# Two attention blocks: layer 1's value product by halves twice, and the late differences of the exponentials moved

## The chip, the cores and the metric

The kernel runs on one core of one Trainium2 chip. The metric is the device time of one execution in microseconds (us); a kernel is given by the median of its runs. A core has five engines that run side by side and wait for each other through semaphores: TensorE (PE, matmuls, into the accumulator memory PSUM), VectorE (DVE), ScalarE (ACT), GpSimd (POOL[...]) and SyncE (SP, which here issues the DMAs).

## What is computed

Eight images of 512 channels and 32 x 32 = 1024 positions ("tokens") go through two attention blocks one after the other. The reference, cut to what matters:

```python
# layer 0: 8 heads of 64 channels, group norm over 32 groups
h = group_norm(x, gn_weight, gn_bias)
q, k, v = split(einsum('oc,bct->bot', w_qkv, h) + b_qkv)      # by head
weight = softmax(einsum('bct,bcs->bts', q * scale, k * scale))
x = x + einsum('oc,bct->bot', w_proj, einsum('bts,bcs->bct', weight, v)) + b_proj
# layer 1: one head of 512 channels, group norm over 8 groups
xn = group_norm(x, gamma, beta)
q, k, v = (conv1x1(xn, w, bias) for w, bias in ((q_w, q_b), (k_w, k_b), (v_w, v_b)))
attn = softmax(einsum('bqc,bck->bqk', q^T, k) * c ** -0.5)
x = x + conv1x1(einsum('bqk,bkc->bqc', attn, v^T)^T, p_w, p_b)
```

All is float32.

## The kernel before

**Products by halves.** Most large products use a Winograd form of Strassen's scheme: both factors are cut into 2 x 2 blocks, seven products of sums of blocks take the place of eight, and the results are added up on the way out of PSUM. `left_sums` (L151) and `right_sums` (L165) make the sums of a left and a right factor. `wino` (L227) runs one such level: steps 1, then 6, 2, 5, 7, then 4 and 3. Steps 4 and 3 are put into the list `tail` and run by `finish` (L223) after step 1 of the next product, so that results are not waited for. `conv2` (L503) divides in halves twice: seven outer products, each of seven inner ones, 49 instead of 64. It takes the outer products in four pairs, (1, 5), (2, 6), (7,), (3, 4), and `inner_steps` (L434) runs the inner steps 1, 6, 2, 5, 7 of a pair, and 3 and 4 as its tail after the next pair's step 1. In the later pairs the results of earlier ones are added in (`x`), and in the third pair POOL adds blocks of the output to each other (`more`, L534).

**PSUM.** Three tags, a, b and c, have two buffers each. In `inner_steps` steps 1 and 2 of a pair share one buffer of a, steps 6, 7 and 4 one of b, steps 5 and 3 one of c. Step 6 adds onto a copy of step 1's result; DVE or ACT must have read b after step 6 before step 7 adds to it.

**Layer 1.** The query and key weights are multiplied into one matrix m, the value and projection weights into one matrix z, in the prologue. For each image `layer1_scores` (L997) forms g = m x image by `conv2`. `layer1_rest` (L1007) then does three stages:

1. `scores1` (L666): the scores by halves twice. DVE evicts, ACT takes the exponential in place (`exps`, L695), POOL adds up the exponentials (`add_up`, L699; the result is `total`). Eight difference operations on whole tiles of exponentials (`steps` of `right_sums`; in the profile `t<-e,e`, `t<-e,t` and `e<-e,e` on L742) make the right factor of the values. The first four run on DVE, the last four on POOL.
2. z: `by_token` (L361), one level of halves, tokens on the partitions. A step has eight matmuls with 256 moving columns. Its weight sums are one tile `w_z`. Hooks after its steps hold the next group norm's mean (`gmean`, `d`, `dv`) and its scale (`gvar`, `ve`), and `sums`, which multiplies `total` with ones, inverts it (`rc`) and sends it round by DMA as rows `r`.
3. `values1` (L746): exponentials times z, one level of halves, with 512 moving columns. It ends with the residual and the store. During this stage the next image's factors `inner_h` are made on POOL and `t_h` on DVE.

**What sets the order.** TensorE's instructions stay in the program's order. Small operations wait in a list `background`; `run_background` takes one per inner step, or a few per step of `wino`. The eight difference operations are put on that list by the last product of the scores, whose tail runs behind z's step 1. Operations that are not pinned may be moved within their engine by the scheduler[...].

**Layer 0's v** is made by the same `conv2` with `by_tokens=True` from the second image on.

**Weights.** The sums of one level are kept in DRAM by `keep` (one DMA), those of two levels by `keep2`, which first makes four more sums (on POOL, `prepare_...` 128x896) and then stores seven parts. `load_weight` loads the next weight tile of a fixed list `uses`; three tiles fit. p and z are prepared during the first image's attention of layer 0.

The lines that matter most:

```python
            def step(j):
                ...
                elif j == 6:
                    mm(ps["b"], 6, False)
                    put([keep_tmp("u2", "u")], "b", (0, 1))
                ...
                elif j == 7:
                    mm(ps["b"], 7, False)
```

Of the kernel before, what the change touches and what calls it, by code (L numbers as in the profile page):

```python
# [9 lines left out]
F32 = mybir.dt.float32  # L10
# [5 lines left out]
P = 128  # L16
EPS = 1e-5
ORDER = (1, 5, 2, 6, 7, 3, 4)
NBIG = 32

# [7 lines left out]
def two_attention_blocks_kernel(  # L30
# [8 lines left out]
    nc = tc.nc  # L39
    B, C, T = x.shape  # L40
    KC = C // P
    HT = T // 2
# [41 lines left out]
    dram = ctx.enter_context(tc.tile_pool(name="dram", bufs=1, space=bass.MemoryType.DRAM))  # L84
# [91 lines left out]
    def main_path(ctx):  # L176
# [8 lines left out]
        def big_tile(name, shape=(P, T)):  # L185
            return big.tile(list(shape), F32, tag="big", name=name)

        def pair_tile(name):
            return big_tile(name, (P, 2, HT))
# [23 lines left out]
        background = []  # L213
# [76 lines left out]
        def keep(n, t):  # L290
            nc.sync.dma_start(wdram[n], t)


        wdram2 = {n: dram.tile([P, 7, 7, P], F32, name=f"sums2_{n}") for n in "qkmv"}

        def keep2(n, t, engine=nc.gpsimd):

# [16 lines left out]
        twice = {n: [(n, 0), (n, 1)] for n in wdram2}  # L314
        layer0 = [*twice["v"], *twice["k"], *twice["q"]]
        uses = ["p", *layer0] if B > 1 else ["p"]
        for b in range(1, B):
            uses += ["p", *twice["m"], "z"] + (layer0 if b + 1 < B else [])
        uses += [*twice["m"], "z"]
        loaded = []  # L320

        def load_weight():
# [18 lines left out]
        def weight(n):  # L341
            return weight_factors(weight_part(n))
# [323 lines left out]
        def scores1(f, gf, gsteps, first, uid, stats):  # L666

            scale = C**-0.5
            e = {(c, cc, r): pair_tile(f"e_{uid}_{c}{cc}{r}") for r in range(2) for c in range(2) for cc in range(2)}
            total = pair_tile(f"sum_{uid}")
            parts = [pair_tile(f"sum{r}_{uid}") for r in range(2)]
            g2 = {1: first}

            def factors(p):
                g2[p] = query_factors(gf[p], f"{p}_{uid}")

            def blocks(at, r, cc):
                return [e[at[1], cc, at[0]][:, :, ts(r, 2 * P)]]

            def add(dst, ps, x):
                nc.vector.tensor_add(dst[0], ps, x[0])  # L685

            def more(dst, x, y, r, cc):

                tc.keep_in_program_order(
                    nc.gpsimd.tensor_tensor(blocks(dst, r, cc)[0], blocks(x, r, cc)[0], blocks(y, r, cc)[0], ALU.add)  # L690
                )

            def exps(r, c):
                for cc in (1, 0):
                    nc.scalar.activation(e[c, cc, r], e[c, cc, r], AF.Exp, scale=scale)  # L695

            def add_up(r, c):

                on = lambda dst, x, y: lambda: tc.keep_in_program_order(nc.gpsimd.tensor_tensor(dst, x, y, ALU.add))  # L699
                if r == c:  # L700
                    return [on(parts[r], e[c, 0, r], e[c, 1, r])]
                return [
                    *(on(parts[r], parts[r], e[c, cc, r]) for cc in range(2)),
                    on(total[:, r, :], parts[r][:, 0, :], parts[r][:, 1, :]),
                ]

            def product(s, p, y, x, before, small, after7=(), final=()):
                def mm(ps, j, start):
                    for i in range(2):
                        matmul(  # L710
                            ps[:, i, :], f[p][j][:, ts(i, P)], g2[p][j], start=start and i == 0, stop=True, skip_group_check=True
                        )

                def extra(r, cc, read, written):

                    if p == 6 and written:
                        more((0, 1), (1, 0), (1, 1), r, cc)
                    if p == 7 and written:
                        more((1, 1), (1, 0), (1, 1), r, cc)

                inner_steps(
                    f"{uid}_{s}", s % 2, 2, mm, add, lambda *at: blocks(y, *at), x and (lambda *at: blocks(x, *at)),
                    extra, after7, final, [lambda: background.extend(small), *(lambda q=q: factors(q) for q in before)],
                )

            product(0, 1, (1, 0), None, [2], stats[:3] + gsteps[:2])
            product(1, 2, (0, 0), (1, 0), [5], gsteps[2:4], (), [lambda: exps(0, 0)])
            product(2, 5, (1, 1), None, [6, 4], gsteps[4:] + stats[3:5])
            product(3, 6, (1, 0), (1, 0), [7, 3], [])
            product(4, 7, (1, 0), (1, 0), [], stats[5:7])  # L730
            product(5, 3, (0, 1), (0, 1), [], stats[7:10] + add_up(0, 0), [lambda: exps(1, 1)], [lambda: exps(0, 1)])
            product(
                6, 4, (1, 0), (1, 0), [], stats[10:] + add_up(1, 1) + add_up(0, 1), (),
                [lambda: exps(1, 0), lambda: background.extend(add_up(1, 0) + steps)],
            )

            t = [[pair_tile(f"t{n}_{uid}_{cc}") for cc in range(2)] for n in (1, 2, 4)]
            engines = [nc.vector] * 4 + [nc.gpsimd] * 4
            fs, steps = right_sums(
                [(e[0, cc, 0], e[0, cc, 1]) for cc in range(2)], [(e[1, cc, 0], e[1, cc, 1]) for cc in range(2)],  # L740
                [lambda cc, n=n: t[n][cc] for n in range(3)],
                lambda *a: engines.pop(0).tensor_tensor(*a, ALU.subtract),  # L742
            )
            return total, {p: [x[:, i, :] for x in fs[p] for i in range(2)] for p in fs}

        def values1(b, zf, ef, r, xt, uid, hooks):  # L746
            def mm(p, i, ps, start):
                for k in range(4):
                    matmul(
                        ps, zf[p][k // 2][:, k % 2, ts(i, P)], ef[p][k], start=start and k == 0, stop=k == 3, skip_group_check=True  # L750
                    )

            def done(i, row, c, ps, u):
                oc = 2 * row + i
                o = upool.tile([P, HT], F32, tag="o", bufs=2, name=f"o_{uid}_{oc}_{c}")
                if u is None:
                    nc.vector.tensor_mul(o, ps, r[:, c, :])
                else:
                    nc.vector.tensor_add(o, ps, u)  # L759
                    nc.vector.tensor_mul(o, o, r[:, c, :])  # L760
                xh = xt[oc][:, ts(c, HT)]
                nc.vector.scalar_tensor_tensor(xh, o, obias[1][:, oc : oc + 1], xh, ALU.add, ALU.add)
                nc.sync.dma_start(out[b, oc * P : (oc + 1) * P, ts(c, HT)], xh)

            wino(f"av_{uid}", mm, done, middle=(2, 5, 6, 7), hooks=hooks, back=4)
# [60 lines left out]
        def prologue():  # L826
# [3 lines left out]
            first = {n: prepare(n) for n in "vqk"}  # L830
# [40 lines left out]
            norm1.affine(acc_tile("gvar_0_1")[:, :KC])  # L871
            bias = bias_products([(wk, "bq1"), (raw_p, "bv1"), (raw_p0, "bv0")])
            later = []
            for n in "pz":
                t, steps = prepare(n)
                later.append(steps)
                later.append([lambda n=n, t=t: keep(n, t), load_weight])
            later.append([
                lambda: tc.keep_in_program_order(nc.vector.tensor_copy(ubias, bias[0])),
                lambda: tc.keep_in_program_order(nc.vector.tensor_add(obias[1], bias[1], pcols("bp1"))),  # L880
# [125 lines left out]

        def layer1_rest(b, inner, gf, gsteps, stats, hooks, ahead):  # L1007
            first = query_factors(gf[1], f"1_1_{b}")
            total, ef = scores1(inner, gf, gsteps, first, f"1_{b}", stats)
            state = {}  # L1010

            def sums():
                state["r"] = reciprocals(total, f"1_{b}", True)

            z = by_token(
                weight("z"), hf, f"z1_{b}", hooks=[*hooks, [sums]], back=3,
                after=[load_weight, lambda: background.extend(zsteps)],
            )
            all_background()
            xt = [load_again(b, c, "x") for c in range(KC)]  # L1020
            stiles = [big_tile(f"sz{i}_{b}", (P, 2, 2, C // 2)) for i in (1, 2, 4)]
            halves = lambda t: (t[:, :, : C // 2], t[:, :, C // 2 :])
            zf, zsteps = left_sums(
                [halves(t) for t in z[:2]], [halves(t) for t in z[2:]],
                [lambda j, t=t: t[:, j, :, :] for t in stiles], nc.vector.tensor_add, nc.vector.tensor_sub,
            )
            values1(b, zf, ef, state["r"], xt, f"1_{b}", ahead)

        for b in range(B):
# [39 lines left out]
            if b > 0:  # L1069
# [5 lines left out]
                else:  # L1075
                    h, loads, applies = begun(load_again, norm1, b, "h1")
                    ahead = [loads, *([f] for f in applies)]
                layer1_rest(b - 1, inner, gf, gsteps, stats, [[], mean, [], affine], ahead)
                if b + 1 < B:
                    v, norm0 = values(b + 1, made["inner"])  # L1080
                    q, k = keys_and_queries(b + 1, made["inner"], norm0, ())
# [219 lines left out]
```

## Time and profile before

| | |
|---|---|
| runs of the kernel before | 2831.85, 2832.86, 2833.0 us; median 2832.86 |
| profiled execution | 2831.03 us, of which the span is 2829.2 us |
| z of the second image, start to the values' first matmul | 534.50 to 554.60 us |
| z's two late steps, after the values' first step | 561.57 to 568.48 us |
| the same, start to values, in the other images | 20.10 us, in the last 19.66 us |
| layer 0's v of the third image, from its first pair's step 6 to its last pair's step 7 | 610.57 to 630.11 us |

The profile's page gives busy time by engine, the chain of work that ended last, and groups of instructions as "line engine operation out<-in (partitions x elements) count | busy us, mean ns of one | idle before it". In a timeline the first column is the start in us from the span's start, the second the time from the first instruction's start to the last one's end of a row, "xN" the number of instructions, and what stands in brackets is the engine's idle time before them and what ended it. In a row of the view of stretches the columns are the stretch, its length, busy time (with the number of instructions) of PE, PE's weight loads, DVE, ACT and POOL, the granted TensorE clock, the DMA share and GB/s. A matmul in float32 leaves two records, and records overlap at their ends, so the pace is read from the distance of starts.

### The profile page before, as it was taken

To read this page: it belongs to the slowest core of one execution; us is meant where nothing else is said; L and a number is where in the kernel's file an instruction comes from. 1 tells how busy PE (TensorE), PEld (TensorE's weight loads), DVE (VectorE), ACT (ScalarE), POOL (GpSimd) and SP (SyncE) were. 2 spreads that over 40 slices of the span, in tenths; PEclk is the share of its full clock that TensorE was granted. 3 is DMA by queue.
4 is the path that set the end of the run, shared out by engine and by line. 5 is a ranking of instruction groups with operands and counts; after the bars stand their busy time and mean duration, and the time that the engine had idled before them with its cause. 6 is when DMAs were issued, how large, how long until landed. Compare 5 with 4: busy or idle time off the path is not lost.

```text
span 2829.2 us, 33980 instructions
## 1 busy us (share of the span) xinstructions
PE 2811.2 (99%) x12434; PEld 1691.7 (60%) x12434; DVE 2119.0 (75%) x2877; ACT 942.7 (33%) x1205; POOL 1250.6 (44%) x1249
## 2 busy tenths in 40 slices
PE   9999999999999999999999999999999999999998
PEld 5435635866367653677537674376843868338584
DVE  5588687766877778777787667877678776887765
ACT  1252452214522145221552215422154312633130
POOL 2214215842267421674117731277223772147672
PEclk9999999999999999999999999999999999999999
DMA  8634403043031330323212232123311224112301
GB/s 286 210 114 147 151 19 121 26 178 138 20 139 53 146 129 23 131 99 119 110 49 105 101 141 90 49 102 123 139 70 49 102 112 158 35 53 95 119 5 68
DMA packets 98850, 291.68 MB, mean 103 GB/s; under 512 B 10803, under 2 KB 42867, under 8 KB 88950
## 3 DMA queue, kind: packets, MB, share of 16 engines
q1 hardware_dynamic: 96886, 287.16, 28.3%
q10 hardware_dynamic: 1792, 2.29, 0.3%
q8 instruction: 100, 1.64, 0.2%
q14 instruction: 72, 0.59, 0.1%
HBM read 236.94 MB, written 52.47 MB: 102 GB/s over the span
## 4 chain that ended last, share of the span: by engine, by line
PE 97%; DVE 1%; issue 1%; POOL 0%; ACT 0%; DVEq 0%; POOLq 0%
PE sc L67 16%; PE av L67 16%; PE psb_av L67 6%; PE psb L67 5%; PE psa_av L67 4%; PE psc_av L67 4%; PE psc L67 3%; PE psa L67 3%; PE psb_z L67 3%; PE psb_p L67 3%; PE psb_k L67 3%; PE psb_g L67 3%; PE psb_v L67 3%; PE psb_q L67 2%; PE psa_p L67 2%; PE psa_z L67 2%
## 5 line engine op out<-in xcount | busy, mean ns | idle before, releaser
L639 DVE TENSOR_TENSOR sum<-sum,e 128x1024 f32<-128x1024 f32 x384 | 518.9, 1351 | 40.7 <-ACT e L635 0.9
L635 ACT ACTIVATE e<-sc 128x1024 f32<-128x1024 f32 x512 | 476.0, 1054 | 79.1 <-PE sc L67 79.1
L67 PE MATMUL sc<-q,k 64*128 64x512 f32 x2048 | 456.8, 596 | 0.0
L67 PE MATMUL av<-e,v 128*64 128x512 f32 x2048 | 453.6, 595 | 0.0
L67 PEld LDWEIGHTS sc<-q,k 64*128 64x128 f32 x2048 | 191.6, 186 | 238.5 <-ACT e L635 109.2
L67 PEld LDWEIGHTS av<-e,v 128*64 128x64 f32 x2048 | 141.4, 137 | 304.3 <-issue 304.3
L601 POOL TENSOR_TENSOR all_recs<-all_recs,rc 128x256 f32<-128x256 f32 x72 | 63.8, 887 | 541.3 <-DVE rc L599 541.3
L658 POOL TENSOR_TENSOR a<-a,r 128x512 f32<-128x512 f32 x56 | 114.9, 2051 | 261.7 <-DMA r<-rows 245.5
L599 DVE RECIPROCAL rc<-sums 128x256 f32<-128x256 f32 x72 | 126.5, 1756 | 46.7 <-PE sums L67 25.3
L653 ACT COPY a<-av 128x512 f32<-128x512 f32 x64 | 37.4, 585 | 321.9 <-PE av L67 321.9
L637 DVE TENSOR_TENSOR sum<-e,e 128x1024 f32<-128x1024 f32 x64 | 78.8, 1231 | 57.0 <-ACT e L635 57.0
L67 PE MATMUL psb<-inner,inner_h 128*128 128x256 f32 x448 | 116.1, 382 | 0.8
L67 PE MATMUL psa_av<-e,z 128*128 128x512 f32 x256 | 113.3, 595 | 0.0
L416 POOL TENSOR_TENSOR inner_h<-h,inner_h 128x256 f32<-128x256 f32 x120 | 107.5, 897 | 3.4
L140 ACT ACTIVATE h<-h,b,s 128x1024 f32<-128x1024 f32 x62 | 78.5, 1270 | 88.0 <-DMA h<-in_x 70.4
L67 PEld LDWEIGHTS psb<-inner,inner_h 128*128 128x128 f32 x448 | 83.9, 190 | 16.6 <-POOL inner L431 3.5
L464 ACT COPY psb_v<-psa_v 128x512 f32<-128x512 f32 (+1 forms) x28 | 14.5, 517 | 227.0 <-DVE o L759 144.6
L416 POOL TENSOR_TENSOR inner_h<-h 128x256 f32<-128x256 f32 x60 | 55.6, 926 | 77.4 <-ACT h L140 77.4
L699 POOL TENSOR_TENSOR sum<-sum,e 128x1024 f32<-128x1024 f32 x32 | 76.1, 2378 | 27.1 <-ACT e L695 25.9
L67 PE MATMUL psb_g<-inner_h,w_m 128*128 128x256 f32 x336 | 85.9, 383 | 0.3
L685 DVE TENSOR_TENSOR e<-psc,u 128x512 f32<-128x512 f32 x56 | 38.7, 691 | 59.0 <-PE psc L67 58.6
L537 POOL TENSOR_TENSOR v<-v,v 128x256 f32<-128x256 f32 x28 | 20.0, 726 | 141.8 <-DVE u_v L532 141.8
(361 smaller groups left out, 5749.6 us busy)
## 6 DMA issues: line engine op xcount, KB each, us to landing
x<-in_x SPq DMA_DIRECT2D x36, 512.0 KB
h<-in_x SPq DMA_DIRECT2D x32, 512.0 KB
spill<-x SPq DMA_DIRECT2D x32, 512.0 KB
h<-spill SPq DMA_DIRECT2D x32, 512.0 KB
x<-spill SPq DMA_DIRECT2D x32, 512.0 KB
out<-x SPq DMA_DIRECT2D x64, 256.0 KB
w_p<-sums_p SPq DMA_DIRECT2D x8, 1792.0 KB
r<-rows SPq DMA_DIRECT2D x112, 128.0 KB
```

The costliest lines, as they stand in the source:

```text
L67: tc.keep_in_program_order(nc.tensor.matmul(*args, **kw))
L140: tc.keep_in_program_order(nc.scalar.activation(dst, src, AF.Identity, bias=b, scale=s))
L416: pin(nc.gpsimd.tensor_tensor(dst, x, y, ALU.subtract))
L599: nc.vector.reciprocal(rc, sums)
L601: nc.gpsimd.tensor_tensor(all_recs, all_recs, rc, ALU.add)
L635: nc.scalar.activation(e, sc, AF.Exp, scale=(C // 8) ** -0.5)
L637: nc.vector.tensor_add(total, es[0], e)
L639: nc.vector.tensor_add(total, total, e)
L653: nc.scalar.copy(dst, av)
L658: nc.gpsimd.tensor_tensor(dst, dst, r, ALU.mult)
L685: nc.vector.tensor_add(dst[0], ps, x[0])
L699: on = lambda dst, x, y: lambda: tc.keep_in_program_order(nc.gpsimd.tensor_tensor(dst, x, y, ALU.add))
```

## The change

z is made by `conv2` with tokens on the partitions, as layer 0's v is: 49 inner products of two matmuls with 128 moving columns, instead of 56 matmuls with 256. Its weight sums are prepared by `keep2` and come as two loads. The values' left sums are taken from halves of the four tiles that `conv2` leaves, and `values1` indexes them so. Of the eight differences of exponentials the first four (the DVE ones) stay on the list behind the scores; the last four are put on the list behind the values' own sums, in z's tail. The mean's hook comes after step 7 of the first pair, the scale's after step 7 of the second, `sums` after step 7 of the third. The pool of large tiles has 33 buffers instead of 32.

```diff
-NBIG = 32
+NBIG = 33
...
-        wdram2 = {n: dram.tile([P, 7, 7, P], F32, name=f"sums2_{n}") for n in "qkmv"}
+        wdram2 = {n: dram.tile([P, 7, 7, P], F32, name=f"sums2_{n}") for n in "qkmvz"}
...
-            uses += ["p", *twice["m"], "z"] + (layer0 if b + 1 < B else [])
-        uses += [*twice["m"], "z"]
+            uses += ["p", *twice["m"], *twice["z"]] + (layer0 if b + 1 < B else [])
+        uses += [*twice["m"], *twice["z"]]
...
-                [lambda: exps(1, 0), lambda: background.extend(add_up(1, 0) + steps)],
+                [lambda: exps(1, 0), lambda: background.extend(add_up(1, 0) + steps[:4])],
...
-            return total, {p: [x[:, i, :] for x in fs[p] for i in range(2)] for p in fs}
+            return total, {p: [x[:, i, :] for x in fs[p] for i in range(2)] for p in fs}, steps[4:]
...
-                        ps, zf[p][k // 2][:, k % 2, ts(i, P)], ef[p][k], start=start and k == 0, stop=k == 3, skip_group_check=True
+                        ps, zf[p][i][:, ts(k, P)], ef[p][k], start=start and k == 0, stop=k == 3, skip_group_check=True
...
-            for n in "pz":
+            for n, store in ("p", keep), ("z", keep2):
                 t, steps = prepare(n)
                 later.append(steps)
-                later.append([lambda n=n, t=t: keep(n, t), load_weight])
+                later.append([lambda n=n, t=t, store=store: store(n, t), load_weight])
...
-            z = by_token(
-                weight("z"), hf, f"z1_{b}", hooks=[*hooks, [sums]], back=3,
-                after=[load_weight, lambda: background.extend(zsteps)],
+            z = conv2(
+                "z", inner, None, f"z1_{b}", [*hooks[:2], [*hooks[2], sums], hooks[3]],
+                after=[lambda: background.extend(zsteps + esteps)], by_tokens=True,
             )
             all_background()
             xt = [load_again(b, c, "x") for c in range(KC)]
-            stiles = [big_tile(f"sz{i}_{b}", (P, 2, 2, C // 2)) for i in (1, 2, 4)]
-            halves = lambda t: (t[:, :, : C // 2], t[:, :, C // 2 :])
+            stiles = [pair_tile(f"sz{i}_{b}") for i in (1, 2, 4)]
+            halves = lambda i, h: (z[i][:, ts(h, HT)], z[2 + i][:, ts(h, HT)])
...
-                layer1_rest(b - 1, inner, gf, gsteps, stats, [[], mean, [], affine], ahead)
+                layer1_rest(b - 1, inner, gf, gsteps, stats, [mean, affine, [], []], ahead)
```

More of the change, by code (lines that the diff above doesn't have):

```diff
@@ L1008, in layer1_rest @@
             first = query_factors(gf[1], f"1_1_{b}")
-            total, ef = scores1(inner, gf, gsteps, first, f"1_{b}", stats)
+            total, ef, esteps = scores1(inner, gf, gsteps, first, f"1_{b}", stats)
             state = {}
@@ L1020, in layer1_rest @@
             xt = [load_again(b, c, "x") for c in range(KC)]
-            stiles = [big_tile(f"sz{i}_{b}", (P, 2, 2, C // 2)) for i in (1, 2, 4)]
-            halves = lambda t: (t[:, :, : C // 2], t[:, :, C // 2 :])
+            stiles = [pair_tile(f"sz{i}_{b}") for i in (1, 2, 4)]
+            halves = lambda i, h: (z[i][:, ts(h, HT)], z[2 + i][:, ts(h, HT)])
             zf, zsteps = left_sums(
-                [halves(t) for t in z[:2]], [halves(t) for t in z[2:]],
-                [lambda j, t=t: t[:, j, :, :] for t in stiles], nc.vector.tensor_add, nc.vector.tensor_sub,
+                [halves(i, 0) for i in range(2)], [halves(i, 1) for i in range(2)],
+                [lambda j, t=t: t[:, j, :] for t in stiles], nc.vector.tensor_add, nc.vector.tensor_sub,
             )
```

## The prediction

> **What bounds the kernel now.** I read the page's busy rows and its chain of waits first.
>
> ```profile
> PE 2811.2 (99%) x12434; PEld 1691.7 (60%) x12434; DVE 2119.0 (75%) x2877; ACT 942.7 (33%) x1205; POOL 1250.6 (44%) x1249
> PE 97%; DVE 1%; issue 1%; POOL 0%; ACT 0%; DVEq 0%; POOLq 0%
> ```
>
> TensorE (PE) is the bound and hardly ever idle: PE work that is saved comes straight off the time, and every PE wait is added to it. So I read PE's timeline through the product z of the second image (its stage starts at 534.50):
>
> ```profile
> 534.50 3.62 PE L67 MATMUL psa_z<-w_z,h 128*128 128x256 f32 x16
> 539.68 3.62 PE L67 MATMUL psb_z<-w_z,t_h 128*128 128x256 f32 x16
> 543.13 0.28 PE L67 MATMUL gmean<-mv,gm 128*128 128x4 f32 x2
> ...
> 554.60 7.13 PE L67 MATMUL psa_av<-e,z 128*128 128x512 f32 x16
> ```
>
> and through layer 0's v, which has the form that z gets, with its row of the view of stretches:
>
> ```profile
> 615.93 1.95 PE L67 MATMUL psb_v<-w_v,inner_h 128*128 128x128 f32 x16
> 617.72 0.61 PE L67 MATMUL psa_v<-w_v,h 128*128 128x128 f32 x4
> ```
>
> ```profile
> 610.57:630.11 19.54, 19.54 (x174) 19.36 (x173) 14.11 (x31) 3.84 (x7) 5.65 (x8) 1.00 0.37 126
> ```
>
> Starts, not durations, give the pace (every matmul leaves two records): 16 records of 256 columns from 539.68 to 543.13 are 0.216 us each; 16 of 128 columns from 615.93 to 617.72 are 0.112. The last row is v from its first pair's second step to its fourth pair's fifth: 19.54 us, PE busy throughout, VectorE (DVE) for 14.11.
>
> Then DVE and GpSimd (POOL) beside z, in the timeline of each:
>
> ```profile
> 544.39 2.29 DVE L119 TENSOR_TENSOR d<-d 128x4 f32<-128x4 f32 x1
> 546.72 0.16 DVE L121 TENSOR_TENSOR dv<-d,mv 128x4 f32<-128x4 f32 x1
> 546.80 3.44 DVE L742 TENSOR_TENSOR t<-e,e 128x1024 f32<-128x1024 f32 x2
> 550.16 6.66 DVE L742 TENSOR_TENSOR t<-e,t 128x1024 f32<-128x1024 f32 x2
> ...
> 556.82 0.68 DVE L238 TENSOR_TENSOR w_z<-psb_z,t_z 128x512 f32<-128x512 f32 x1
> ```
>
> ```profile
> 541.89 4.78 POOL L699 TENSOR_TENSOR sum<-sum,e 128x1024 f32<-128x1024 f32 x2 [2.51 <-ACT e L695]
> 546.75 1.27 POOL L699 TENSOR_TENSOR sum<-sum 128x512 f32<-128x512 f32 x1
> 549.18 6.56 POOL L742 TENSOR_TENSOR e<-e,e 128x1024 f32<-128x1024 f32 x2 [1.17 <-DVE t L742]
> ```
>
> A 128x4 operation (d) takes 2.29 us, just until POOL's sum ends; its like dv takes 0.16. The second two t's take 3.3 us each, together with POOL's two e's; the second t of 546.80 met no POOL operation and took 1.2. So the two engines take turns. From gmean (544.01) to the eviction w_z (556.82) DVE is shut for 12.8 us, while the matmuls that w_z reads ended at about 552. PE does not feel it today: each of three PSUM tags has two buffers and a step lasts 3.45 us.
>
> [...] This trace shows it once, after 3.7 us of idle at the start:
>
> ```profile
> L70 PE MATMUL tr_wk<-ident,rawk 128*128 128x128 f32 x16 | 3.4, 401 | 3.7 <-DMA rawk<-in_w 3.7
> L70 PE MATMUL tr_wv<-ident,rawv 128*128 128x128 f32 x16 | 2.1, 276 | 0.5 <-DVE k L392 0.5
> ```
>
> The same 16 transposes cost 1.3 us more there, though the clock column says 1.00.
>
> **What is saved.** z has 7 products x 8 matmuls x 2 records x 0.216 = 24.2 us per image. New: 49 products x 2 matmuls x 2 records x 0.112 = 21.9. That is 2.2 us in each of 8 images, 17.8 in all, if nothing waits.
>
> **Where PE will wait.** Times are from z's start. PE runs the first pair's step 1 (0 to 0.9), the scores' two late steps (to 2.6), steps 6, 2, 5, 7 (to 6.35), gmean, the second pair's step 1 (to 7.4), the first pair's 3 and 4 (to 9.2), and the second pair's 6, 2, 5 (to 11.9). The second pair's step 7 adds into the bank that step 6 filled, so DVE must have taken u_z out of it first. In the changed program's order of instructions DVE has ahead of that u_z: the step 7 eviction of the first pair, t, gmean, t, d, the step 3 eviction, d, t, dv, t. The t's were there before too. New is that an eviction which PE asks for within two steps of 0.9 us stands behind them.
>
> The scores' tail comes 2.55 us earlier, and so do the two exponentials on ScalarE (ACT) that start at 5.31 now. POOL's sums then begin at 4.9 (two of 2.35, one of 1.27), and its two e's follow (2.35 each). DVE evicts step 7 from 6.6 to 7.3 and starts the first t at 7.35. [...]t to 8.6, sum to 10.8, t to 11.9, sum to 13.05, e to 15.45 (d waits behind both), t to 16.6, e to 18.9, t to 20.1. As a check: POOL 2.35 + 1.27 + 2 x 2.35 = 8.3 and four t's 4.6 are 12.9, the 12.8 of now. u_z, two operations of 0.42, ends at 20.9. PE resumes at 21.0 after 9.1 us of idle.
>
> After that the evictions keep up, as in v: until the values DVE has about 8 us of 256- and 512-column evictions (0.42 and 0.69), rc 1.75 and low_recs 0.47, in 11.3 us. POOL's eight added z sums (0.73 each, v's row) find it idle; three stand behind all_recs, which waits for rc, and I count them as in time. Step 7 to the values is 19.54, less 80 records of 0.112 up to step 7, plus gvar 0.14 and sums 0.57: 11.3 us. At half pace for 3 us PE loses 1.5. So the values start at 33.8 instead of 20.1 (554.60), and z's own two late steps behind the values' first step take 1.8 instead of 6.9: 33.8 + 1.8 - 20.1 - 6.9 = 8.6 us more per image. The last image has no mean in the queue; there t follows t, the fourth ends at 17.5, PE resumes at 18.4, the values start at 31.1 instead of 19.65: 6.3. Together 7 x 8.6 + 6.3 = 66.5.
>
> **The other edits.** The last two t's on POOL (2.35 each) move behind z's sums and four inner_h into the values' stage, where only a late step reads them: 0, hidden by some 40 us of matmuls; 4.8 per image without that cover. w_z comes as two loads of 1.8 and 1.4 MB instead of one, DMA being busy for about a quarter, ahead of its use as before: 0. A 33rd buffer: 0. The mean's hooks move by a step or two: in the schedule above. Once, in the first image's attention, POOL gets four prepare_z operations of 2.08 us (prepare_q's row) against DVE's running sums of 1.23: taking turns, DVE ends a sum at 167.8 instead of 161.1, and PE asks for it at 162.8. That is 5.0 us, 5.5 with part of a slow restart. The seven small stores on SP's queue stand before rows of attention that nothing on PE's path reads soon: 0.
>
> Sum: 66.5 + 5.5 = 72 on the profiled execution's 2831.0 (span 2829.2); with the median, 2832.9 + 72 = 2905.
>
> **Rivals.** (1) The stall is there but smaller: PE restarts at full pace (8 x 1.5 less) and attention hides its adds (5.5 less), 2887; if also the d operations slip between POOL's, 2.6 less in seven images, 2869. For it: the first d, at 544.20, took 0.16. Against: the second took 2.29. (2) Faster: the t's do not hold u_z, it is out by 11.9 and the saving stays, 2833 - 18 = 2815. It decides below 2.2 us of stall per image. For it: v runs without a wait. Against: v has neither t's in its queue nor sums on POOL. (3) Larger: the fourth pair's evictions wait for POOL's sums behind all_recs (1.5), and the slow restart lasts twice as long (1.5): 8 x 3 = 24 more, 2929.
>
> **Numbers.** Main 0.60, smaller 0.20, larger 0.13, faster 0.05, no change 0.02 (0.2% is about what a measurement of this kernel can tell). The range goes from the far end of the smaller case to the start of the larger one: 2868 to 2927. Slower holds all but the last two.
>
> **What would show it.** Right: in each z a PE idle of 7 to 9 us before the second pair's psb_z, ended by DVE u_z, with t's of 1.2 to 3.4 us ahead of it; matmuls at twice the spacing behind it; in attention 0 a sums matmul that waits for DVE. Wrong: no PE idle inside z, or idle only before the fourth pair.

## The result, and the profile after

The changed kernel takes 2933.47 us (median of four runs, 2932.79 to 2937.74) against 2832.93 before: a ratio of 1.0359, with a 95% interval of 1.0341 to 1.0377. Its profiled execution has a span of 2931.6 us, 102.4 more than before. The loss was forecast, and so was its main part, the stall in z. The time is 28 us above the forecast of 2905 and 6.5 above the end of the range.

Two lines of the page of the changed kernel, busy rows and chain of waits, and then the group of z's matmuls:

```profile
PE 2821.8 (96%) x13106; PEld 1716.3 (59%) x13106; DVE 2196.5 (75%) x3037; ACT 956.9 (33%) x1237; POOL 1311.0 (45%) x1317
PE 90%; DVE 8%; issue 2%; ACT 0%; POOL 0%; DVEq 0%; POOLq 0%; ACTq 0%
...
L67 PE MATMUL psb_z<-w_z,inner_h 128*128 128x128 f32 x672 | 97.7, 295 | 64.4 <-DVE u_z L532 64.4
```

PE was busy 99% of the span, now 96%. Though z has fewer columns to move, PE's busy time grew by 10.6 us: matmuls behind a stall ran at half pace (0.21 us a record in place of 0.11, below), and they count as busy. DVE's share of the chain went from 1% to 8%. What PE waits for, over the whole run (us in total, times, the longest):

```profile
PE psb_z L67 <- DVE u_z L532: 64.4, 8, 8.3
PE psb_av L67 <- DVE u_av L238: 11.3, 4, 3.0
PE psb L67 <- DVE e L685: 7.0, 8, 1.2
PE sums L67 <- DVE sum L639: 4.8, 1, 4.8
PE tr_wk L70 <- DMA rawk<-in_w: 3.7, 1, 3.7
PE psb_av L67 <- DVE w_av L238: 2.1, 1, 2.1
```

`u_av` and `w_av` are DVE's evictions after steps 6 and 7 of the values, `e` is one of the scores, `sum` the running sum of an attention. Only the 3.7 us of `tr_wk` was there before, and of the third row 0.5. The first and the fourth row are the waits that the prediction named; the waits for u_av, e and w_av are not in it.

The stall in z of the second image, in the timelines of DVE, POOL and PE (its stage starts at 544.23):

```profile
551.37 1.27 DVE L742 TENSOR_TENSOR t<-e,e 128x1024 f32<-128x1024 f32 x1
...
552.64 3.29 DVE L742 TENSOR_TENSOR t<-e,e 128x1024 f32<-128x1024 f32 x1
555.86 1.22 DVE L117 TENSOR_TENSOR d<-mv,gmean 128x4 f32<-128x4 f32 x1
...
557.60 1.77 DVE L119 TENSOR_TENSOR d<-d 128x4 f32<-128x4 f32 x1
559.30 1.21 DVE L742 TENSOR_TENSOR t<-e,t 128x1024 f32<-128x1024 f32 x1
560.44 2.29 DVE L121 TENSOR_TENSOR dv<-d,mv 128x4 f32<-128x4 f32 x1
562.65 1.21 DVE L742 TENSOR_TENSOR t<-e,t 128x1024 f32<-128x1024 f32 x1
563.79 0.74 DVE L532 TENSOR_TENSOR u_z<-psb_z,z 128x256 f32<-128x256 f32 x2
```

```profile
549.20 5.65 POOL L699 TENSOR_TENSOR sum<-sum,e 128x1024 f32<-128x1024 f32 x2
554.93 2.12 POOL L699 TENSOR_TENSOR sum<-sum 128x512 f32<-128x512 f32 x1
557.02 5.69 POOL L742 TENSOR_TENSOR e<-e,e 128x1024 f32<-128x1024 f32 x2
```

```profile
564.58 2.08 PE L67 MATMUL psb_z<-w_z,inner_h 128*128 128x128 f32 x8 [8.33 <-DVE u_z L532]
...
567.73 1.06 PE L67 MATMUL psc_z<-w_z,h 128*128 128x128 f32 x4
568.59 1.06 PE L67 MATMUL psc_z<-w_z,t_h 128*128 128x128 f32 x4
...
570.97 0.61 PE L67 MATMUL psa_z<-w_z,h 128*128 128x128 f32 x4
571.42 0.61 PE L67 MATMUL psc_z<-w_z,inner_h 128*128 128x128 f32 x4
```

`u_z`, two operations that take 0.74 together, stands behind four full-tile differences and three 128x4 operations, which cost 0.16 alone and here 1.2 to 2.3. The fourth difference starts at 562.65, just as POOL ends its last operation (562.71): the operations of the two had taken turns. PE resumes 20.35 us after z's start (forecast 21.0). The distance of starts shows the half pace: four records take 0.86 us from 567.73 and 0.45 from 570.97, so 0.21 a record in place of 0.11, for 5.3 us. The granted clock beside it (the column of 0.50 in this row of stretches) says the same; it is 1.00 up to 559.6 and again from 569.84:

```profile
559.60:569.83 10.23, 5.25 (x24) 5.25 (x25) 7.16 (x12) 0.36 (x1) 4.73 (x5) 0.50 0.00 0
```

Where the 102.4 us lie, from the starts of PE's stages in the two traces. The rows "z and values" run from z's first matmul to the first of the next stage:

| stage | measured | forecast |
|---|---|---|
| prologue | +0.7 | 0 |
| first image's attention (0.25 of it in another image's) | +7.8 | +5.5 |
| scores, 8 images | +8.4 | 0 |
| z and values, three images without a wait for u_av | +8.2, +8.3, +8.3 | +8.6 each |
| z and values, four images with one | +13.8, +14.2, +11.5, +10.8 | +8.6 each |
| z and values, last image | +7.7 | +6.3 |
| the stages behind the values (v, g) | +2.7 | 0 |

The two columns add up to 102.4 and 72.0. So z, where nearly all of the working was, came out within half a microsecond in the images that nothing else disturbed (1.4 in the last), and 30 us came from elsewhere: about 20 from the values and the stage behind them (1.8 of these from a longer half pace in z of the first two images), 8 from the scores, 2 from the attention.

### The profile page after: what moved, and what is told of

Read it like the earlier page. It is cut to its first block, busy times and chain, and to the rows that moved or that the text cites. A ratio compares the mean times of both kernels' runs of the same rounds, so it can differ in the third digit from the quotient of the medians.

```text
span 2931.6 us, 35720 instructions
## 1 busy us (share of the span) xinstructions
PE 2821.8 (96%) x13106; PEld 1716.3 (59%) x13106; DVE 2196.5 (75%) x3037; ACT 956.9 (33%) x1237; POOL 1311.0 (45%) x1317
## 3 DMA queue, kind: packets, MB, share of 16 engines
q10 hardware_dynamic: 1792, 2.29, 0.2%
## 4 chain that ended last, share of the span: by engine, by line
PE 90%; DVE 8%; issue 2%; ACT 0%; POOL 0%; DVEq 0%; POOLq 0%; ACTq 0%
PE sc L67 15%; PE av L67 15%; PE psb L67 5%; PE psb_av L67 5%; PE psa_av L67 3%; PE psc L67 3%; PE psa L67 3%; PE psc_av L67 3%; PE psb_p L67 3%; PE psb_k L67 3%; PE psb_g L67 3%; PE psb_v L67 3%; PE psb_z L67 3%; PE psb_q L67 2%; PE psa_p L67 2%
## 5 line engine op out<-in xcount | busy, mean ns | idle before, releaser
L639 DVE TENSOR_TENSOR sum<-sum,e 128x1024 f32<-128x1024 f32 x384 | 526.0, 1370 | 40.7 <-ACT e L635 0.9
L658 POOL TENSOR_TENSOR a<-a,r 128x512 f32<-128x512 f32 x56 | 107.6, 1921 | 261.9 <-DMA r<-rows 244.2
L67 PE MATMUL psb_z<-w_z,inner_h 128*128 128x128 f32 x672 | 97.7, 295 | 64.4 <-DVE u_z L532 64.4
L67 PEld LDWEIGHTS psb_z<-w_z,inner_h 128*128 128x128 f32 x672 | 89.2, 207 | 67.3 <-DVE u_z L532 66.1
L416 POOL TENSOR_TENSOR inner_h<-t_h 128x256 f32<-128x256 f32 x90 | 89.9, 1004 | 23.9 <-DVE t_h L170 23.9
L140 ACT ACTIVATE h<-h,b,s 128x1024 f32<-128x1024 f32 x62 | 78.7, 1270 | 21.6 <-DMA h<-in_x 14.2
```

The costliest lines, as they stand in the source:

```text
L67: tc.keep_in_program_order(nc.tensor.matmul(*args, **kw))
L140: tc.keep_in_program_order(nc.scalar.activation(dst, src, AF.Identity, bias=b, scale=s))
L416: pin(nc.gpsimd.tensor_tensor(dst, x, y, ALU.subtract))
L639: nc.vector.tensor_add(total, total, e)
L658: nc.gpsimd.tensor_tensor(dst, dst, r, ALU.mult)
```

## The experiments

**1. The late differences alone.** The kernel before with the one edit:

```diff
-                [lambda: exps(1, 0), lambda: background.extend(add_up(1, 0) + steps)],
+                [lambda: exps(1, 0), lambda: background.extend(add_up(1, 0) + steps[:4])],
...
-                after=[load_weight, lambda: background.extend(zsteps)],
+                after=[load_weight, lambda: background.extend(zsteps + esteps)],
```

> The kernel before, with the late differences alone. Theory[...]: waits of PE for u_av of 0.5 to 3 us appear in some images, 2836 to 2855. Rival (lost cover): no PE idle in the values, 2831 to 2835.

2866.02 us (2860.46 to 2870.06), ratio 1.0124 (1.0107 to 1.0141). So the edit that the prediction priced at nothing costs 1.2% of the kernel by itself, with z as it was. The waits of PE, and then DVE and POOL in the values of the second image:

```profile
PE psb_av L67 <- DVE u_av L238: 15.7, 4, 4.3
PE psb_av L67 <- DVE w_av L238: 4.2, 1, 4.2
```

```profile
580.35 2.34 DVE L170 TENSOR_TENSOR t_h<-h 128x512 f32<-128x512 f32 x2
582.61 2.83 DVE L172 TENSOR_TENSOR h<-h,h 128x512 f32<-128x512 f32 x1
585.37 3.96 DVE L171 TENSOR_TENSOR t_h<-h,t_h 128x512 f32<-128x512 f32 x2
```

```profile
582.10 5.54 POOL L742 TENSOR_TENSOR t<-e,t 128x1024 f32<-128x1024 f32 x2
```

POOL's two t's lie just on DVE's h and t_h. One h took 2.83 us, where none in the kernel before takes over 1.21, and u_av comes after them on DVE. DVE has no idle time in these rows, so it waits for no load there. The waits that the theory expected are there, and the rival falls. Their size was put too small (up to 3 us, and 2855): the five waits are 3.3 to 4.3 us, and the mean granted clock of the profiled run is 0.996 (0.999 before).

**2. The late differences undone.** The changed kernel with all eight on the list behind the scores again:

```diff
-                [lambda: exps(1, 0), lambda: background.extend(add_up(1, 0) + steps[:4])],
+                [lambda: exps(1, 0), lambda: background.extend(add_up(1, 0) + steps)],
...
-            return total, {p: [x[:, i, :] for x in fs[p] for i in range(2)] for p in fs}, steps[4:]
+            return total, {p: [x[:, i, :] for x in fs[p] for i in range(2)] for p in fs}, []
```

> The late differences alone are undone: all eight stand behind the scores again, the rest is as in the changed kernel. Theory (the two t's moved on POOL meet DVE's sums in the values' stage[...]): the PE waits for u_av and w_av there, 13.4 us of idle over six images and some 2 us of slow restart each, are gone, the 8.3 us in each z stay: 2908 to 2920. Rival (the values lost the cover of z's late steps, 1.8 us instead of 6.9): the waits for u_av stay within a third, 2928 to 2938.

2931.81 us (2931.78 to 2931.84), ratio 1.0352 (1.0331 to 1.0372): no gain. The waits for u_av are gone, as the theory says, and another has taken their place:

```profile
PE psb_av L67 <- DVE w_av L238: 13.6, 6, 2.4
```

Neither expectation was met. DVE's timeline shows what was late:

```profile
612.05 0.69 DVE L238 TENSOR_TENSOR w_av<-psb_av,t_av 128x512 f32<-128x512 f32 x1
...
613.50 7.14 DVE L760 TENSOR_TENSOR o<-o,r 128x512 f32<-128x512 f32 x1
...
621.35 0.68 DVE L238 TENSOR_TENSOR w_av<-psb_av,t_av 128x512 f32<-128x512 f32 x1
```

POOL's timeline beside it, two rows of a run of inner_h that goes on without a gap:

```profile
613.22 0.73 POOL L416 TENSOR_TENSOR inner_h<-h,h 128x256 f32<-128x256 f32 x1
613.90 0.73 POOL L416 TENSOR_TENSOR inner_h<-h,inner_h 128x256 f32<-128x256 f32 x1
```

A multiplication with both inputs in SBUF took 7.14 us instead of 0.69. POOL was not in one long operation: nine short ones went past, and DVE got no turn between them. The second w_av, which PE waits for, comes after it (621.35). Six of the 48 such multiplications took 6.2 to 7.1 us, and there are six waits. In the changed kernel this happened once (6.55 us, in the last image), and that is its wait of 2.1 for w_av.

**3. The same, with the evictions ahead.** To see whether DVE lacks time in the values or only has the wrong thing in front, both step 7 evictions were put before the two outputs:

```diff
+                            tc.keep_in_program_order(nc.vector.tensor_add(u3[i], ps["b", i], t1[i]))
...
+                if p == 7 and uid.startswith("av"):
+                    for i in range(2):
+                        done(i, 1, 1, ps["c", i], u3[i])
```

> The changed kernel with the late differences undone, and in step 7 of the values both evictions w_av put ahead of the two outputs that DVE multiplies by r. Theory (DVE is shut out[...] by POOL's row of inner_h without a gap, and the second w_av waits only because it stands behind the multiplication that is shut out): the multiplication still takes 6 to 7 us in six images, but PE's waits for w_av fall from 13.6 us to under 1.5, and with the slow matmuls behind them the time falls from 2931.8 to 2908 to 2916 us. Rival (DVE is short of time in the values' stage, wherever an eviction stands): PE waits 8 us or more for DVE there, 2925 to 2934 us.

2910.88 us (2908.93 to 2913.23), ratio 1.0282 (1.0264 to 1.0299). Waits for w_av and for u_av are both gone, as the theory had it; the longest that is left is that of z:

```profile
PE psb_z L67 <- DVE u_z L539: 64.4, 8, 8.4
```

The multiplications are still held up, though they take only 3.2 to 4.1 us in seven places, less than expected: they come later in POOL's row. DVE has the time; what counts is which operation the one held up stands in front of. With this and the late differences undone, 22.6 us of the changed kernel's time are gone, which is the 20 of the table within the spread of the runs.

**4. The late differences moved further on.** The changed kernel with POOL's two t's put behind fourteen inner_h and pinned there, and the evictions of step 7 ahead as in experiment 3. The lines for the t's:

```diff
-                after=[lambda: background.extend(zsteps + esteps)], by_tokens=True,
+                after=[lambda: background.extend(zsteps + esteps[:2])], by_tokens=True,
...
+            ahead = list(ahead) + [[] for _ in range(5 - len(ahead))]
+            ahead[3].append(lambda: ahead[4].extend(esteps[2:]))
             values1(b, zf, ef, state["r"], xt, f"1_{b}", ahead)
```

> The changed kernel with the two last differences on POOL moved on, behind fourteen of POOL's inner_h, and with the step 7 evictions ahead of the outputs' multiplications. Theory (the two differences hold DVE[...] while it has the values' own sums and t_h in its queue ahead of u_av): PE's waits for u_av fall from 11.3 us to under 2 and those for w_av from 2.1 to under 1; 2906 to 2915 us. Rival (z's shorter late steps leave DVE too little time in front of u_av, whatever POOL does): waits for u_av stay at 7 us or more, 2922 to 2935 us.

2962.72 us (2961.85 to 2964.22), ratio 1.0463 (1.0446 to 1.0481): the slowest of all, and neither expectation. PE's waits, and DVE between the two u_av:

```profile
PE psb_av L67 <- DVE u_av L238: 35.6, 5, 7.2
```

```profile
604.70 0.69 DVE L238 TENSOR_TENSOR u_av<-psb_av,t_av 128x512 f32<-128x512 f32 x1 [1.47 <-PE psb_av L67]
617.26 0.69 DVE L98 BATCH_NORM_STATS2 bnst<-ahead 128x6 f32<-128x512 f32 x1 [11.87 <-DMA ahead<-in_x]
617.88 0.67 DVE L238 TENSOR_TENSOR u_av<-psb_av,t_av 128x512 f32<-128x512 f32 x1
```

The first u_av is on time, as the theory said: DVE waited 1.47 us for PE there. But a statistic of the next image's x now stands between the two u_av, and it waits 11.87 us for its load. That load takes a large buffer, and the t's, run at 611.4 to 616.1 here, keep the exponentials that they read in theirs. What the queue that issues these loads (L209) waits for, from 595 to 625, names them:

```profile
SPq L209 <- POOL t L749: 17.9, 2, 16.1
```

The load reads nothing that a t writes, so what it waits for is the buffer. The first is issued at 613.78, when the first of the two t's has ended, and the statistic starts 3.5 us later. A late operation costs what it holds DVE up, and here also the buffers that its inputs take: the load waited up to 16.1 us for one.

**5. The late differences in an idle slot.** The t's put directly behind z's sums, where POOL is idle for eleven microseconds in the changed kernel (578.7 to 589.9) and DVE for most of them, with the evictions of step 7 ahead.

```diff
-                after=[lambda: background.extend(zsteps + esteps)], by_tokens=True,
+                after=[lambda: [f() for f in esteps], lambda: background.extend(zsteps)], by_tokens=True,
```

> The changed kernel with the two last differences on POOL put directly behind its z sums, ahead of the values' own sums, where POOL and DVE are both idle for some 8 us, and with the step 7 evictions ahead of the outputs' multiplications. Theory (the late differences cost what they hold[...] while DVE has the values' sums and t_h in its queue): PE's waits for u_av fall from 11.3 us to under 1 and those for w_av from 2.1 to under 1; 2906 to 2915 us, as with the late differences undone. Rival (z's shorter late steps leave DVE too little time in front of u_av, whatever POOL does): waits for u_av of 7 us or more, 2922 to 2935 us.

2915.15 us (2912.49 to 2915.84), ratio 1.0292 (1.0276 to 1.0308). The list of PE's waits has none for u_av or w_av any more. With experiments 2 and 3 this settles the values: z's shorter late steps, the rival here and in experiments 2 and 4, are the same in all of these kernels and bring no wait for u_av, and the late differences cost what they take from DVE at the place where they were put.

**6. All differences behind z.** All eight, in turn with the values' own sums, four on DVE and four on POOL. This takes the differences out of z.

```diff
-                after=[lambda: background.extend(zsteps + esteps)], by_tokens=True,
+                after=[lambda: background.extend([f for i in range(0, 8, 2) for f in (*zsteps[i : i + 2], *esteps[i : i + 2])])], by_tokens=True,
```

> All eight differences of exponentials go behind z, each pair of them after the pair of the values' own sums that the same step needs; nothing else differs from the changed kernel. Theory (the four t's on DVE stand in front of the second pair's u_z[...]): the 8.3 us of PE idle in each z goes to under 0.5 us and with it the slow restart, 64 + 17 us in all; the t's now load DVE in the values' stage, where 0 to 6 us per image may come back: 2850 to 2895. Rival (z by halves twice cannot be evicted in time at this place, t's or not): 7 us or more of idle stay in each z, 2920 to 2940.

2919.1 us (2918.11 to 2922.11), ratio 1.0306 (1.0288 to 1.0323). The u_z wait is gone, as the theory had it, but the time is just below the rival's range:

```profile
PE psb_av L67 <- DVE u_av L238: 53.5, 8, 7.6
PE psb_av L67 <- DVE t L742: 8.9, 6, 1.5
...
PE psc_av L67 <- DVE t L742: 5.0, 7, 0.7
```

The 64.4 us for u_z are gone, so it is the differences that hold u_z. But 67.4 us of waits stand in the values in their place. The stall moved: DVE's differences and sums were again beside POOL's differences (one pair of `sz` took 5.57 us beside POOL's two t's).

**7. One more large buffer.** `NBIG = 34`, and one buffer instead of two for the reciprocals and their rows (to make room).

```diff
-NBIG = 33
+NBIG = 34
...
-        rpool = ctx.enter_context(tc.tile_pool(name="rpool", bufs=2))
+        rpool = ctx.enter_context(tc.tile_pool(name="rpool", bufs=1))
```

> The changed kernel with 34 large buffers (room for it comes from one instead of two buffers for rc and r in attention, which may cost there). Theory (the new PE wait for DVE's e in the scores, 0.9 to 1.2 us in seven images, is a wait for a large buffer, since the factors of the image are now held through z): it goes, 7 us of idle and about 1 us more, 2922 to 2928 if attention keeps its pace. Rival (a change of order on DVE or POOL makes it): it stays, 2932 to 2936.

2931.83 us, the median of two that lie far apart (2926.67 and 2937.0), so only its trace is read:

```profile
PE psb_z L67 <- DVE u_z L532: 64.1, 8, 8.3
PE sums L67 <- DVE sum L639: 8.9, 2, 4.8
```

The row `psb <- DVE e` is back at the 0.5 us of the kernel before, and the scores take as long as before the change (0.0 us in all, against +8.4). The buffers are the cause there. What takes them is z's new form and not the late differences: the row stands at 7.0 in experiment 2, without these, and at 0.5 in experiment 1, with them alone. As the program reads, z now uses the image's seven inner factors, so they live on through the scores. A second wait in the attention came in the same trace, with the single reciprocal buffers. PE's wait for u_av came down from four images to two (5.4 us); why is open.

**8. The additions in the attention apart.** The four for z one at a time, with an empty hook between them.

```diff
+            tz, steps = prepare("z")
+            ops, store = keep2_parts("z", tz)
+            later += [steps, ops[:1], [], ops[1:2], [], ops[2:3], [], [ops[3], store, load_weight]]
```

> The changed kernel with POOL's four additions for z in the first image's attention taken apart, each in a hook of its own with an empty one between. Theory[...]: PE's wait of 4.8 us for the sum falls under 1, 2924 to 2930 us. Rival (each addition delays one sum, wherever it stands): waits of 3 us or more in total remain, 2930 to 2937 us.

2931.68 us (2930.55 to 2932.81), ratio 1.0353 (1.0332 to 1.0373), too near to the changed kernel to tell by the time. The trace tells: attention costs +2.9 us instead of +7.8, and the wait is

```profile
PE sums L67 <- DVE sum L662: 2.7, 3, 1.3
```

Each is something between the two expectations: with an addition alone PE still waits up to 1.3 us for a sum, and of the +2.9 us these waits are 2.7, which leaves next to nothing for half pace.

**9. All on POOL, and then a better place for each.** The first form: four differences on POOL behind its sums in z, two behind z's sums, two behind fourteen inner_h; the mean one pair later; step 7 and attention as in 3 and 8.

> All eight differences on POOL: the first four behind its sums in z, the next two behind its z sums, the last two behind fourteen inner_h; the mean's hook one pair later in z; step 7 evictions ahead of the outputs; the four additions for z in the first attention spread over its hooks. Theory[...]: no PE wait for u_z, u_av, w_av or the running sums over 2 us in total each, and what stays is the scores' wait, some 10 us, against a saving of 17.8: 2822 to 2845 us. Rival (POOL's queue becomes the late one, so that PE or DVE waits for its differences or its z sums in every image): 2850 to 2910 us.

2927.01 us (2925.92 to 2928.21), ratio 1.0337 (1.0319 to 1.0354), far from the theory's number and above the rival's. The values have the late load of experiment 4 (33.1 us for u_av). And in z there is no difference left on DVE, but still a stall of 5.4 us:

```profile
552.78 2.12 DVE L117 TENSOR_TENSOR d<-mv,gmean 128x4 f32<-128x4 f32 x1
554.93 2.27 DVE L119 TENSOR_TENSOR d<-d 128x4 f32<-128x4 f32 x1
557.23 2.26 DVE L121 TENSOR_TENSOR dv<-d,mv 128x4 f32<-128x4 f32 x1
```

Three operations on four columns hold DVE for 6.7 us, each for about the length of one of POOL's (2.3 to 2.4 us). So four differences at 1.15 us on DVE are not needed for a stall: one POOL operation beside each small one was enough. The last image, which has no mean in z, has no such stall.

The second form moves the mean to z's third pair, where POOL has operations of 0.73 us, and the last four differences directly behind z's sums. The third adds the edit of experiment 7. The second's edits, those of 3 and 8 and the pins of POOL's differences left out:

```diff
-            engines = [nc.vector] * 4 + [nc.gpsimd] * 4
+            engines = [nc.gpsimd] * 8
...
-                after=[lambda: background.extend(zsteps + esteps)], by_tokens=True,
+                after=[lambda: [f() for f in esteps], lambda: background.extend(zsteps)], by_tokens=True,
...
-                layer1_rest(b - 1, inner, gf, gsteps, stats, [mean, affine, [], []], ahead)
+                layer1_rest(b - 1, inner, gf, gsteps, stats, [[], [], mean, affine], ahead)
```

> All eight differences on POOL: four behind its sums in z, four behind its z sums; the mean's hook in z's third pair and the scale's in the fourth, where POOL's operations are short; step 7 evictions ahead of the outputs; the four additions for z in the first attention apart. Theory[...]: no wait for u_z over 1 us, none for u_av or w_av, and what stays is the scores' wait, some 10 us, and 3 us in the first attention, against the 17.8 us saved: 2822 to 2836 us, at or just below the kernel before. Rival (POOL's list becomes the late one): PE waits of 3 us or more in each image, 2845 to 2890 us.

> The same with 34 large buffers and one buffer instead of two for each of the reciprocals and their rows. Theory: the scores' wait of 0.8 to 1.2 us an image goes too, with the slow matmuls behind it, and the single buffers cost at most one wait of some 4 us in the first attention: 2812 to 2828 us, under the kernel before. Rival (the buffers bring back in the attentions what they save in the scores): within 3 us of the kernel with 33 buffers.

The second: 2835.14 us (2833.33 to 2838.04), ratio 1.0011 (1.0005 to 1.0018). The third: 2825.14 us (2824.43 to 2827.69), ratio 0.9977 (0.9968 to 0.9987), 7 us below the kernel before. Both lie in the theory's range, the second at its end and 3 us above the kernel before. The third's waits that are new:

```profile
PE psb_z L67 <- DVE u_z L562: 4.0, 7, 0.6
PE sums L67 <- DVE sum L669: 2.8, 3, 1.3
```

This is the same arithmetic as the changed kernel, with 108 us less. Six of its multiplications by r still take 6.0 to 6.5 us, and PE feels none of them. The saving of 17.8 us shows in part: z and values give back about 13 us over the eight images, with 0.6 us of idle left in front of u_z in seven of them, and the attention and v, 3 us more each, take almost half of that again.

## Why the prediction went wrong, step by step

- **The stall in z: right, mechanism and size.** Cause, place and order on DVE were as written: u_z ran at 563.79, after the four t's and the three small operations. Resumption 20.35 against 21.0, values 33.6 to 35.0 against 33.8 in the first seven images; 31.2 against 31.1 in the last. Experiments 6 and 9 carry the cause: without the differences on DVE in z the wait for u_z goes (6) or shrinks (to 5.4 us in 9's first form), and there DVE's small operations beside POOL's are what is left.
- **"At half pace for 3 us PE loses 1.5": too small.** The 3 us were an estimate, and they fit the start of the trace before, where the records lie 0.21 us apart from 3.74 to 6.60 and 0.11 from 6.79. In the changed kernel, after the same 8.3 us of idle, the half pace lasted 5.3 and 6.5 us in the first two images (a loss of 2.8 and 3.4) and 3.3 to 4.0 in the other five (a loss of about 2). The last section shows what went with the length. In z the earlier resumption balanced it, but for 0.6 and 1.2 us in the first two images; in the attention (4.85 us of idle and 2.7 of slow matmuls, against 5.0 and 0.5) nothing did, which is most of the 2 us there. The prediction also notes that the clock column says 1.00 in the half pace at the start: the clock's record in that trace begins at 6.75 us, when this half pace ends (the column counts the time before it as 1.00). In the stalls of the changed kernel it reads 0.50.
- **"The last two t's on POOL move ... : 0, hidden by some 40 us of matmuls": wrong, and the largest miss.** Some 20 us. The matmuls do hide the t's themselves; PE waited for them in no image of the changed kernel. What was missed is what DVE does meanwhile. The working for z had used that a DVE operation beside one of POOL's takes longer (a t of 3.3 us in place of 1.2, a d of 2.29 in place of 0.16); the same was not asked in the values, where more than ten DVE operations of that kind come before u_av. Experiment 1 gives the edit's price alone, 1.2%; experiments 3 and 5 take it away.
- **"A 33rd buffer: 0": wrong.** 8.4 us in the scores. The edit was read as room added. What it is added for counts too: z by `conv2` reads the seven inner factors, so they stay through the scores, and 33 are too few where 34 are enough. Experiment 7 and the step from the second to the third form in 9 show it (scores +8.0 to +0.3).
- **The loads of w_z, the stores on SP's queue, POOL's z sums: 0, right.** No wait for any of them is in the trace.
- **The rivals.** "Smaller" and "faster" fell with the stall's size. "Larger", 2929, was near in time only: of its two terms the fourth pair's wait did not come, and the longer half pace in z came to some 6 us over the eight images where it had 12.

## What to carry to other kernels

Two operations of POOL that were moved under matmuls cost 1.2% here (experiment 1), though PE never waited for them. Before a move between DVE and POOL, go through what the other of the two has to run there, and what PE needs that comes after that. Count the buffers that the moved and the rerouted data keep alive, at the point of their last reader, not of their first. When DVE is late, look first at what stands in front of the eviction; putting the eviction ahead, or a small operation next to POOL's short ones, gained more here than any saved matmul.

## What the runs showed of the hardware

- **DVE beside POOL.** Some of DVE's operations took longer beside POOL's, and one of POOL's beside DVE's. In z the two took turns: a 128x4 operation of 0.16 us took up to 2.29, just until POOL's ended. In the values a DVE operation of 0.69 us took 7.14, while nine of POOL's ran with no gap between them (experiment 2), and at 599.16 in experiment 4 a POOL operation of 0.72 took 4.65 while DVE ran six of 0.64. What decides between turns and being shut out was not found.
- **Half pace.** In the trace of the changed kernel the granted clock goes to 0.50 eleven times while PE has work, and stays there for 3.41, 6.83 or 10.24 us. All its changes lie whole multiples of 3.413 us apart, within 0.01 us (559.60, 569.84, 610.80 and 614.21: 3, 12 and 1 times). Divide the trace at these multiples into stretches, and add up PE's idle time in each (gaps over 0.2 us): the eleven stretches at full clock with 2.07 us or more of it were each followed by 0.50, and none with 1.90 or less was. (The first stretch, before the clock's record begins at 6.64 us, and the end, after PE's last matmul, are left out.) Other runs need not have the same limit: in experiment 2 a stretch with 1.81 us was followed by 0.50. How a wait lies to these stretches made the difference. The same two waits of 0.65 and 1.16 us, in v of the second image, halve the clock in experiment 2, where both fall into one stretch:

```profile
270.34:273.74 3.40, 1.59 (x12) 1.31 (x12) 3.40 (x8) 1.66 (x3) 0.03 (x1) 1.00 1.09 330
273.75:277.15 3.40, 3.40 (x19) 3.40 (x18) 2.25 (x4) 0.23 (x1) 0.00 (x0) 0.50 0.90 311
```

and not in the changed kernel, where they fall into two (the stretch after these is at 1.00 as well):

```profile
269.47:272.87 3.40, 2.75 (x21) 2.28 (x20) 3.40 (x7) 0.59 (x1) 2.37 (x3) 1.00 0.83 308
272.88:276.29 3.41, 2.25 (x20) 2.06 (x19) 2.89 (x7) 1.07 (x2) 0.00 (x0) 1.00 1.05 332
```

The waits for u_av in the changed kernel go the same way. Those of 2.83 and 2.81 us, with 2.74 and 2.81 in one stretch, were followed by half pace (16 records took 8.75 and 8.80 us in place of 7.03). Those of 3.02 and 2.67, with at most 1.59 and 1.79 in one stretch, were not (7.10 and 7.11). The clock came back to 1.00 after stretches with at most 0.11 us of idle and stayed at 0.50 after those with 0.28 or more, and the half pace after one and the same stall of 8.3 us lasted from 3.3 to 6.5 us.
